# Cross attention's maxima and sums by way of memory in eleven of sixteen batches, in a decoder layer on one Trainium2 core

## The chip, the core and the metric

The kernel runs on one core of a Trainium2 chip. The core has five engines with an instruction queue each. TensorE multiplies matrices and writes to PSUM. VectorE, ScalarE and GpSimd work on rows of 128 partitions. SyncE (SP in the profile) does no arithmetic here and only issues transfers. Sixteen DMA engines carry the transfers between the chip's memory (HBM, "memory" from here on) and SBUF, the core's working memory. [...]

The metric is the device time of one execution in microseconds. A profile of one more execution names every instruction with its start and its end. In the profile PE is TensorE's matmuls, PEld its weight loads, DVE is VectorE, ACT ScalarE, POOL GpSimd.

## The reference

One layer of a decoder over x of shape (16, 128, 512), all float32, in three stages that each end in a residual sum and a layer norm:

```python
x = _layernorm(x + _L0_attn_ref(x, ...))              # retention, 16 heads of 32
x = _layernorm(x + _L0_xattn_ref(x, ctx_2048, ..., 64))  # banded cross attention
x = _layernorm(x + _L0_ffn_ref(x, ...))               # 16 routed rows of each batch
```

The second stage is what the change is about. It works on each batch for itself, with the 512 columns as positions and the 128 rows as features, in 8 heads of 16 features:

```python
scores = einsum('bqhd,bkhd->bhqk', q, k) / sqrt(d)
scores = where(abs(q_pos - k_pos) <= 64, scores, neg)
attn = softmax(scores, axis=-1)
o = einsum('bhqk,bkhd->bqhd', attn, v).reshape(n, t, e)
o = transpose(o @ w_out.T + b_out)
y = relu(o) * encodings
out = einsum('nit,io->not', y, w_ct) + b_ct
```

The third stage picks 16 rows of each batch by a router score, runs attention (16 heads of 128, 8 key heads) and a gated feed-forward of width 2048 on the 256 picked rows, and puts them back.

## The kernel before

**Stages and order.** Retention goes in eight groups of two batches: projections `Q`, `K`, `V` and the gate `G` (`rotated` L549, `values` L568, `gates` L577), scores `R` (`retain` L598), their use `Y` (`weigh` L624), the group norm (`variance`, `normalise`) and the output projection `O` (`finish` L667). Cross attention goes in 32 units m: a unit is one batch n and one head group hg of four heads. `start_ff` then frees retention's weights, loads those of the feed-forward, and the last part follows.

The order of all this is written out by hand. `PLACES`, `ENDS`, `FIRST`, `ONCE` and `FF_PLACES` hold a number for each stage of each step ("s0", "low", "w0", "div" ...), in units of which four make a group. `in_order` sorts these numbers and issues the steps in that order; a step that yields is continued at its next number. So the numbers fix each engine's instruction order, the order on the DMA queues too, and nothing else schedules.

**A cross-attention unit.** The four heads of a unit lie at partitions 0, 32, 64 and 96. Of each 32 partitions, 16 hold the head's features (rows 0 to 15 in head group 0, 16 to 31 in group 1), and one of the others is free: `FREE = (16, 0)`.

1. `project` (L689) makes qT and kT of a batch, 128x512, one tile for each head group. The free row of kT holds 1.
2. `scores` (s0, s1): 8 program matmuls for each half of the positions (L719) into four PSUM banks, then eight masked maxima on VectorE (L727), one of each head and 128 positions. Each lands in a column of the tile x_mx (128 positions in the partitions).
3. `lower` (low): the maxima have to stand in the free row of qT, with the positions along the row. Four TensorE transposes of 128x128 against the identity (L738) bring x_mx there, and VectorE forms x_qa = qT - transposed (L740). As the free row of kT is 1, the next product subtracts each position's maximum by itself.
4. `weights` (w0, w1): the same products the other way round (L753), so that the keys are in the partitions, exp on ScalarE (L758), the band cut out on GpSimd (L764).
5. `attend` (av): values times weights (L775). V (`project_v`, x_va) has a column of ones, so that one row of each 32 of the result is the sum of the weights. ScalarE copies it to xu (L780).
6. `divide` (div): four transposes (L788) put the positions into partitions, VectorE takes the sums' reciprocals (L791) and multiplies (L794) into xo.
7. `turn`: when both head groups are there, four more transposes (L801) turn xo back, ScalarE adds the bias b_v (L803).
8. `project_out` (L808, L810, L812), `settle` (L818 to L842: second layer norm, router score, plain output to memory) and `rank` (L853 to L868: which rows are picked).

The eight PSUM banks are one pool, `banks`, which every step above shares. The feed-forward opens pools of its own after it; its first `frot_ps` of the queries (`rotary`, L966; ScalarE L974 and L976, VectorE L972) has to wait until the old banks are read out.

**Queues.** SP issues nearly all transfers in the order of the places: xT and x of a group (`load`), the encodings (`encoder`, L699), the plain output (L842), the weights. ScalarE's queue issues a few at the start. A transfer that waits holds up those behind it on its queue.

## Time and profile before

| what | value |
|---|---|
| three timed runs | 879.86, 881.25, 881.61 us; median 881.25 |
| the profiled execution | 879.75 us, of which the span from first to last instruction is 878.0 |
| granted TensorE clock, mean over the span | 0.993 |
| instructions | 17870 |
| DMA | 51.31 MB, 16 engines busy for 18% of the span |

How it is read: busy time is the union of an engine's instructions. A group's line gives where it stands in the code, engine, operation, what it writes and reads, how often; after the bar the busy time in us and the mean duration of one in ns; after the second bar the engine's idle time just before, and what ended it. Matmuls overlap each other in the pipeline, so a group's busy time is more than the time by which it moves what comes after. float32 matmuls appear as two instructions each, transposes as one. "PEclk" and the column after the five engines in the table by stages are the granted clock of TensorE, 1.00 being full. A DMA line gives the size and the median time from its issue to its landing.

### The profile page before, as it was taken

How to read it: one execution, taken by the hardware profiler on the slowest of the kernel's cores; microseconds unless marked ns; L12 is line 12 of the kernel's file. 1: busy time of each engine (PE TensorE's matmuls, PEld its weight loads, DVE VectorE, ACT ScalarE, POOL GpSimd, SP SyncE). 2: the span in 40 equal slices, each digit the busy share in tenths (PEclk: the TensorE clock that was granted, in tenths of full speed). 3: DMA queues.
4: the chain of work that ended last, by engine and by line, in shares of the span. 5: the costliest groups of instructions: out<-in, count | busy, mean ns of one | idle time of the engine just before them, and what ended most of it. 6: DMA issues, size and time to landing. Idle time of an engine off the chain costs nothing.

```text
span 878.0 us, 17870 instructions
## 1 busy us (share of the span) xinstructions
PE 835.0 (95%) x6940; PEld 582.5 (66%) x6940; DVE 527.6 (60%) x1789; ACT 392.7 (45%) x768; POOL 346.2 (39%) x508
## 2 busy tenths in 40 slices
PE   7999999999999999999999999998988699999996
PEld 5666767766766775677667757565553587658862
DVE  4645665666676777767677877888853256412101
ACT  0323645635555564545456456575532256521100
POOL 2444454355354745544552744446531121000001
PEclk9999999999999999999999999999999899999999
DMA  9500100100001001011000000019100522242500
GB/s 300 171 1 5 58 1 1 62 1 2 26 18 56 13 26 61 13 40 46 3 13 26 13 14 26 13 35 327 36 27 14 190 96 71 74 144 96 187 5 24
DMA packets 29619, 51.31 MB, mean 58 GB/s; under 512 B 4448, under 2 KB 7776, under 8 KB 29536
## 3 DMA queue, kind: packets, MB, share of 16 engines
q1 hardware_dynamic: 27024, 47.81, 16.2%
q10 hardware_dynamic: 2352, 1.84, 0.7%
q8 instruction: 55, 0.90, 0.4%
q0 software_dynamic: 160, 0.52, 0.2%
q14 instruction: 28, 0.23, 0.1%
HBM read 45.45 MB, written 4.72 MB: 57 GB/s over the span
## 4 chain that ended last, share of the span: by engine, by line
PE 83%; DVE 6%; ACT 3%; issue 3%; DMA 2%; POOL 1%; POOLq 0%; ACTq 0%; SPq 0%; DVEq 0%
PE xt_ps L753 7%; PE o_ps L667 6%; PE gu_ps L1154 6%; PE g_ps L577 6%; PE xs_ps L719 6%; PE v_ps L568 6%; PE q_ps L549 6%; PE xav_ps L775 6%; PE k_ps L549 6%; PE down_ps L1166 3%; PE wo_ps L1129 3%; PE xqk_ps L689 3%; PE frot_ps L966 2%; PE ret_ps L598 2%; PE y_ps L624 2%
## 5 line engine op out<-in xcount | busy, mean ns | idle before, releaser
L727 DVE CUSTOM_DVE_ANT_0 x_masked<-xs_ps,x_band 128x192 f32<-128x192 f32 (+1 forms) x512 | 200.1, 391 | 103.1 <-PE xs_ps L719 64.6
L764 POOL TENSOR_SCALAR_AFFINE_SELECT xp_t<-xp_t 128x512 f32<-128x512 f32 (+1 forms) x256 | 142.1, 591 | 101.4 <-ACT xp_t L758 101.3
L758 ACT ACTIVATE xp_t<-xt_ps 128x448 f32<-128x448 f32 x256 | 118.6, 550 | 60.3 <-PE xt_ps L753 60.2
L753 PE MATMUL xt_ps<-x_qa,x_kT 32*128 32x192 f32 (+1 forms) x1024 | 68.5, 374 | 2.0 <-DVE x_qa L740 1.5
L719 PE MATMUL xs_ps<-x_kT,x_qT 32*128 32x192 f32 (+1 forms) x1024 | 68.7, 358 | 1.2 <-ACT x_qT L692 0.6
L549 PE MATMUL q_ps<-xT,w_W_Q 128*128 128x256 f32 x256 | 60.5, 390 | 5.1 <-DMA w_W_Q<-in_W_Q 5.1
L753 PEld LDWEIGHTS xt_ps<-x_qa,x_kT 32*128 32x128 f32 x1024 | 45.2, 184 | 27.7 <-issue 13.0
L577 PE MATMUL g_ps<-xT,w_W_G 128*128 128x256 f32 x256 | 59.4, 385 | 1.6 <-DMA w_W_G<-in_W_G 1.6
L568 PE MATMUL v_ps<-w_W_V,xT 128*128 128x512 f32 x128 | 58.2, 597 | 1.1 <-DVE w_W_V L484 1.1
L549 PEld LDWEIGHTS q_ps<-xT,w_W_Q 128*128 128x128 f32 x256 | 48.8, 194 | 15.6 <-DMA xT<-in_xT 5.0
L549 PE MATMUL k_ps<-xT,w_W_K 128*128 128x256 f32 x256 | 58.6, 382 | 0.0
L667 PE MATMUL o_ps<-w_W_O,y 128*128 128x512 f32 x128 | 58.4, 599 | 0.0
L719 PEld LDWEIGHTS xs_ps<-x_kT,x_qT 32*128 32x128 f32 x1024 | 52.1, 184 | 9.0 <-DVE x_mx L727 3.1
L775 PE MATMUL xav_ps<-xp_t,x_va 128*32 128x192 f32 (+1 forms) x1024 | 55.0, 355 | 1.8 <-DVE rank L865 0.9
L577 PEld LDWEIGHTS g_ps<-xT,w_W_G 128*128 128x128 f32 x256 | 47.4, 190 | 11.5 <-DMA w_W_G<-in_W_G 2.0
L549 PEld LDWEIGHTS k_ps<-xT,w_W_K 128*128 128x128 f32 x256 | 47.9, 190 | 9.4 <-issue 1.6
L608 POOL TENSOR_SCALAR_AFFINE_SELECT rt<-rt 128x2048 f32<-128x2048 f32 x16 | 32.1, 2005 | 54.7 <-ACT rt L603 50.3
L775 PEld LDWEIGHTS xav_ps<-xp_t,x_va 128*32 128x32 f32 x1024 | 31.1, 110 | 21.9 <-issue 6.0
L979 POOL TENSOR_TENSOR other<-other,ff_sin 128x512 f32<-128x512 f32 x12 | 15.4, 1287 | 72.6 <-ACT other L976 72.6
L568 PEld LDWEIGHTS v_ps<-w_W_V,xT 128*128 128x128 f32 x128 | 23.5, 190 | 28.7 <-issue 25.4
L727 DVE DVE_READ_ACCUMULATOR2_ANT x_mx<- 128x1 f32 x512 | 42.4, 83 | 0.0
L667 PEld LDWEIGHTS o_ps<-w_W_O,y 128*128 128x128 f32 x128 | 23.4, 190 | 27.0 <-issue 23.3
(199 smaller groups left out, 1488.2 us busy)
## 6 DMA issues: line engine op xcount, KB each, us to landing
xp<-in_x SPq DMA_DIRECT2D x16, 256.0 KB, 4.4
enc<-in_ctx SPq DMA_DIRECT2D x16, 256.0 KB, 2.6
out<-z_plain SPq DMA_DIRECT2D x16, 256.0 KB, 2.0
wq<-in_wq SPq DMA_DIRECT2D x4, 1024.0 KB, 5.2
wo<-in_wo SPq DMA_DIRECT2D x4, 1024.0 KB, 6.1
w_gate<-in_w_gate SPq DMA_DIRECT2D x4, 1024.0 KB, 5.1
w_up<-in_w_up SPq DMA_DIRECT2D x4, 1024.0 KB, 5.2
w_down<-in_w_down SPq DMA_DIRECT2D x4, 1024.0 KB, 6.0
```

The source lines that it names most:

```text
L549: nc.tensor.matmul(ps[:, i * GT:(i + 1) * GT], w[wname][:, kc, hg * P:(hg + 1) * P], st["xT"][:, kc, :], start=(kc == 0), stop=(kc == KC - 1))
L568: nc.tensor.matmul(ps, state[g]["xT"][:, kc, b * S:(b + 1) * S], w["W_V"][:, kc, :], start=(kc == 0), stop=(kc == KC - 1))
L577: nc.tensor.matmul(ps[:, i * GT:(i + 1) * GT], w["W_G"][:, kc, hg * P:(hg + 1) * P], state[g]["xT"][:, kc, :], start=(kc == 0), stop=(kc = ...
L608: nc.gpsimd.affine_select(out=v, in_=v, pattern=[[0, 8 * GB], [1, S]], base=0, channel_multiplier=-1, compare_op=ALU.is_ge, fill=0.0)
L667: nc.tensor.matmul(ps, st["y"][:, kc, b * S:(b + 1) * S], w["W_O"][:, kc, :], start=(kc == 0), stop=(kc == KC - 1))
L719: nc.tensor.matmul(ps[j][:, OFF[c]:OFF[c] + LEN[c]], qT[hs, c * P:(c + 1) * P], kT[hs, LO[c]:LO[c] + LEN[c]], start=True, stop=True)
L727: nc.vector.tensor_tensor_reduce(out=junk[:, 0:LEN[c]], in0=ps[j][:, OFF[c]:OFF[c] + LEN[c]], in1=band[:, SEEN[c]:SEEN[c] + LEN[c]], scale ...
L753: nc.tensor.matmul(ps[j][:, OFF[c]:OFF[c] + LEN[c]], kT[hs, c * P:(c + 1) * P], qa[hs, LO[c]:LO[c] + LEN[c]], start=True, stop=True)
L758: nc.scalar.activation(p[:, j, :], ps[j][:, 0:448], AF.Exp, scale=XD ** -0.5)
L764: nc.gpsimd.affine_select(out=v, in_=v, pattern=[[0, 4], [sign, b - a]], base=a if sign == 1 else P - a, channel_multiplier=-sign, compare ...
L775: nc.tensor.matmul(ps[32 * j:32 * (j + 1), LO[c]:LO[c] + LEN[c]], va[:, c, hg * 4 + j, :], p[c // 2][:, j, OFF[c]:OFF[c] + LEN[c]], start= ...
L1154: nc.tensor.matmul(ps[:, j * n:(j + 1) * n], loaded[f"{w}{q}"][:, kc, at:at + P], ff["x1", "T"][:, kc, lo:hi], start=(kc == 0), stop=(kc = ...
```

## The change

In batches 2 to 12 (`IN_MEMORY`) the maxima and the sums go to their rows through memory; batches 0, 1, 13, 14 and 15 keep TensorE's transposes.

- `lower`: the maxima are kept as 16 columns of a 128x32 tile. VectorE transposes its 32x32 blocks into x_mT, SP writes that to memory (128 runs of 128 bytes) and, at a later place, reads it back straight into the four free rows of qT (4 rows of 2 KB). qT itself is used in `weights`; there are four qT buffers in place of two and no x_qa. The free row of kT now holds -1, and the batches with transposes add in place of subtracting.
- `attend`: SP writes the four rows of sums to memory. The values of head group 1 stand at rows 16 to 31, and there are three xu buffers in place of one.
- `divide`: SP reads the sums as 32x64, VectorE takes the reciprocals, SP writes them and reads them back spread over 32 partitions each (256 KB, x_rb), VectorE multiplies xu by them and by a mask. Each of the four pieces has a place of its own.
- `turn`: GpSimd adds the two head groups; there is no transpose.
- b_v is folded into the output's bias by one small matmul at the start; w_out and b_v are loaded in eight pieces each, with their rows in the new order. V is copied out of PSUM in two pieces.
- xpos and w_mean stand in tiles that are used later for something else.
- All places are other numbers, the feed-forward's too. TensorE's order in the feed-forward, from the queries on, is the same as before. Just before it, the second batch half's first key block stands ahead of its value block in place of behind it.

The core of the diff, without the numbers:

```diff
+IN_MEMORY = range(2, 13)
...
         def lower(m):
             n, hg = divmod(m, 2)
-            mx = mxs[hg].rearrange("p c j w -> p c (j w)")
-            ps = bank("xmx_ps")
-            for c in range(NQ):
-                nc.tensor.transpose(ps[:, c * P:(c + 1) * P], mx[:, c, :], ident)
-            qa = xk.tile([P, D], F32, name="x_qa")
-            nc.vector.tensor_tensor(qa, cross[n].pop(("q", hg)), ps, ALU.subtract)
-            unit[m] = dict(qa=qa, p={})
+            unit[m] = dict(qa=cross[n].pop(("q", hg)), p={})
+            if n not in IN_MEMORY:
...
+                return
+            mT = small.tile([P, 32], F32, name="x_mT", bufs=2)
+            nc.vector.transpose(mT, mxs[hg])
+            m_d = dram.tile([32, NQ, 32], F32, name="x_mT_d")
+            nc.sync.dma_start(out=m_d.rearrange("jc b q -> b jc q"), in_=mT)
+            yield
+            nc.sync.dma_start(out=unit[m]["qa"][FREE[hg]::32, :],
+                              in_=m_d[0:4 * NQ].rearrange("(j c) b q -> j (c b q)", j=4))
...
-            u = xk.tile([P, D], F32, name="xu", bufs=1)
+            u = xk.tile([P, D], F32, name="xu", bufs=3)
             nc.scalar.copy(u, ps)
             unit[m]["u"] = u
+            if n in IN_MEMORY:
+                sum_d = dram.tile([4, D], F32, name="sum_d")
+                nc.sync.dma_start(out=sum_d, in_=u[FREE[hg]::32, :])
+                unit[m]["sum"] = sum_d
...
         def divide(m):
...
+            few = D // 8
+            r = xk.tile([32, few], F32, name="x_r", bufs=1)
+            nc.sync.dma_start(out=r, in_=unit[m]["sum"].rearrange("j (q k) -> (j q) k", k=few))
+            yield
+            nc.vector.reciprocal(r, r)
+            inv_d = dram.tile([4, D], F32, name="inv_d")
+            nc.sync.dma_start(out=inv_d.rearrange("j (q k) -> (j q) k", k=few), in_=r)
+            yield
+            rb = xk.tile([P, D], F32, name="x_rb", bufs=1)
+            nc.sync.dma_start(out=rb, in_=bc(inv_d, 1, 32))
+            yield
             u = unit.pop(m)["u"]
+            nc.vector.scalar_tensor_tensor(u, u, ours[:, hg:hg + 1], rb, ALU.mult, ALU.mult)
+            cross[n]["o", hg] = u
...
         def turn(n):
+            o = cross[n]["oT"] = xk.tile([P, D], F32, name="xo", bufs=1)
+            if n in IN_MEMORY:
+                nc.gpsimd.tensor_tensor(o, cross[n]["o", 0], cross[n]["o", 1], ALU.add)
+                return
...
+            ps = bank("bias_ps")
+            nc.tensor.matmul(ps[:, 0:1], w_out, b_v, start=True, stop=True)
+            nc.vector.tensor_tensor(b_out, b_out, ps[:, 0:1], ALU.add)
```

## The prediction

> **What bounds the kernel now.** I read the page's busy table and its slices, then the chain that ended last, then the busy time by stages, TensorE's groups and waits, and last the DMA list. Busy times and slices (40 of 21.95 us each):

> ```profile
> PE 835.0 (95%) x6940; PEld 582.5 (66%) x6940; DVE 527.6 (60%) x1789; ACT 392.7 (45%) x768; POOL 346.2 (39%) x508
> PE   7999999999999999999999999998988699999996
> DVE  4645665666676777767677877888853256412101
> PE 83%; DVE 6%; ACT 3%; issue 3%; DMA 2%; POOL 1%; POOLq 0%; ACTq 0%; SPq 0%; DVEq 0%
> ```

> The third line above is VectorE by slices, the fourth the chain by engine. TensorE bounds everything: 83% of the chain, full slices except near the start, at 590 to 700 us and at the end. Stages (us; busy of each engine, then clock):

> ```profile
> 100.00:500.00 400.00, 399.37 (x3893) 278.94 (x3893) 281.69 (x974) 211.31 (x376) 204.28 (x296) 1.00 0.07 23
> 500.00:580.00 80.00, 79.09 (x818) 51.67 (x817) 62.93 (x238) 46.28 (x84) 36.39 (x61) 1.00 0.06 21
> 580.00:650.00 70.00, 61.10 (x636) 38.26 (x635) 55.95 (x217) 39.25 (x74) 40.09 (x74) 1.00 0.35 125
> 650.00:700.00 50.00, 38.09 (x198) 25.47 (x197) 19.04 (x53) 13.93 (x37) 7.91 (x11) 0.91 0.27 90
> ```

> From 100 to 500 us TensorE waits 0.6 us in all, VectorE works 70%. From 580 us on (only cross attention left; I call it the drain) VectorE is at 80% and TensorE idles 9 us; from 650 to 700 it idles 12 us, 8.0 of them in one wait. The transposes, and that wait:

> ```profile
> L738 PE MATMUL xmx_ps<-consts,x_mx 128*128 128x128 f32 x128 | 20.6, 279 | 0.2
> L788 PE MATMUL xut_ps<-consts,xu 128*128 128x128 f32 x128 | 19.8, 278 | 1.1 <-ACT xu L780 1.1
> L801 PE MATMUL xoT_ps<-consts,xo 128*128 128x128 f32 x64 | 9.8, 276 | 0.9 <-DVE xo L794 0.9
> PE frot_ps L966 <- ACT other L976: 9.1, 2, 8.0
> ```

> How four transposes stand in TensorE's time (start, duration):

> ```profile
> 311.81 0.60 PE L738 MATMUL xmx_ps<-consts,x_mx 128*128 128x128 f32 x4
> 312.25 0.60 PE L788 MATMUL xut_ps<-consts,xu 128*128 128x128 f32 x4
> 312.78 0.32 PE L624 MATMUL y_ps<-rt,v 128*32 128x128 f32 x4
> 322.30 0.66 PE L738 MATMUL xmx_ps<-consts,x_mx 128*128 128x128 f32 x4
> 322.79 1.06 PE L706 MATMUL xv_ps<-x_w_v,xp 128*128 128x128 f32 x8
> 331.25 0.60 PE L801 MATMUL xoT_ps<-consts,xo 128*128 128x128 f32 x4
> 331.69 0.59 PE L667 MATMUL o_ps<-w_W_O,y 128*128 128x512 f32 x1
> ```

> Durations overlap; a group of four holds TensorE 0.44, 0.53, 0.49 and 0.44 us from its start to the next group's, mean 0.475.

> **The sum's base.** The profiled execution took 879.75 us (span 878.0, 1.75 around it), 1.5 under the median of the three timed runs.

> **1. Transposes removed.** Eleven batches are 22 units (batch and head group). Each loses four transposes of maxima and four of sums, each batch four in `turn`: 22 x 8 + 11 x 4 = 220, or 55 groups. By starts 55 x 0.475 = 26.1 us; by the rows' busy time 176 x 0.158 + 44 x 0.153 = 34.5 us, which counts overlapped tails. I take 26 and keep 34.5 as the end. One matmul for the bias is added, 0.2 us (nearest: a one-column matmul, 210 ns). [...]

> **2. Other engines, per unit.** VectorE loses the subtraction (L740, 675 ns), the reciprocal (L791, 252) and the product (L794, 424): 22 x 1.35 = 29.7 us. It gains a 32x32-block transpose of 128x32 (bounds 83 ns, the accumulator read, and 220, the 128x128 copy; I take 0.15), a reciprocal of 64 columns (between 252 ns for 16 and 948 for 128; 0.55) and a product of 128x512 out of SBUF (between 0.75, L1143, and twice 0.757, L659 with 256 columns; 1.0, near L834's 0.87): 22 x 1.7 = 37. Net +8 us on 527.6, range +2 to +20: hidden under TensorE until the drain. ScalarE loses eleven evictions of 692 ns and evicts V in two pieces (0 to +0.6 us, 16 times), GpSimd gains eleven additions of 1.3 us; both have over 40% free.

> **3. Memory trips, maxima.** Between the last score matmul and the first `weights` matmul of a unit now lie: eight masked maxima (8 x (0.39 + 0.083) = 3.8 us), the transpose 0.15, two issues on SP (0.34 each) and two landings, the second issued only when the first has landed. No row has such a trip. Bounds from the list of DMAs:

> ```profile
> out<-z_plain SPq DMA_DIRECT2D x16, 256.0 KB, 2.0
> enc<-in_ctx SPq DMA_DIRECT2D x16, 256.0 KB, 2.6
> x_b_k<-in_b_k SPq DMA_DIRECT2D x1, 0.5 KB, 2.9
> xp<-in_x SPq DMA_DIRECT2D x16, 256.0 KB, 4.4
> ```

> A lone one lands in 2.0 to 2.9 us, 4.4 behind others. I take 2.0 to 2.9, since these are small and the engines 5% busy: the chain is 8.6 to 10.4 us, 13.4 at 4.4. Against it I counted, in the changed program's order, the TensorE work that stands in between, by starts: in unit 6 it is eight `rotated` matmuls, eight scores, sixteen `attend`, one output and four `finish`, 10.7 us; in unit 19 10.2; in the other twenty 11.9 to 21.4, the median of all 15.7. So two of 22 units are tight. In the 2nd to 7th groups the waits cost 0 to 3 us; I take 2. Nothing is queued behind a waiting `weights` matmul but all of TensorE, so such a wait counts in full.

> [...]

> **4. Memory trips, sums.** After `attend`: copy 0.59, four hops (the last writes 256 KB: 2.6 to 5.7, the row of w_router), reciprocal 0.55, product 1.0, both groups added 1.3: 13 to 19 us with issues. TensorE work up to the output matmul is 25 to 77 us, except in batch 12's second group: 14. There I take 1 us (0 to 4). On VectorE the reciprocal and the product may wait for their DMA and hold back masked maxima queued behind; a few reciprocals stand only 1 to 2 us after their load's place.

> **5. SP's queue.** 22 x 6 = 132 DMAs and 14 small ones at the start, each 0.34 us of issue, all in one order. Three per unit wait for the DMA before them, 2 to 2.9 us each, so SP is held 4 x (6 x 0.34 + 3 x 2.5) = 38 us of each group of some 80. Behind them stand xT, x, enc and z transfers, each placed many us ahead of its reader; I cost that at nothing. At the start the 14 extra issues (0.43 each) move the last b_v piece from 31 to about 37 us; its matmul comes near 39.

> **6. Places.** Start: R0's scores now precede the gates and the tables precede centring; VectorE and GpSimd rows put R0 at 23.3 us, where 1.65 us were lost before, and V is due at 33.5 as before: 0 (-1 to +2). Join with the feed-forward: the 8.0 us wait was for two evictions of key heads; now one of them has a V block beside it, and the other takes 4 x 1.16 = 4.7 us: -3 (-3.3 to 0). Drain: in the last 131 us of TensorE work before the first queries VectorE has 125 us by rows where it had 118, with 20 us of TensorE idling before; +4 (0 to +12).

> The clock bears on both: the granted clock was 0.91 from 650 to 700 us, and a `fv` block that began at 673.28, after waits of 2.11 and 0.78, took 8.83 us where its twin took 7.03. The waits between 40 and 650 us, all under 1.0 us, left it at 1.00. So a wait of some 2 us can cost 1.8 more; one such is inside the +4 of the drain. [...]

> **Sum:** 879.75 - 26.1 + 0.2 + 2 + 1 - 3 + 4 = 857.9; taken as 858.

> **Rivals.** *A. Memory slower than the gaps, ends slower.* The chain of step 3 grows to C, and a unit waits C less its gap. Summed over the 22 gaps that is 1 us at 11, 3 at 12, 16 at 14 and 25 at 15: from C = 15 the saving is eaten. That needs hops of 5 us, or VectorE or SP lagging by 5. For it: the 4.4 us row, SP held for half of its time, VectorE at 70 to 80%. Against: 2.0 to 2.9 alone. At 5.5 us a hop C is 15.6 and the stalls are 31 us in place of my 2: 887. *B. Drain bound by VectorE:* its end of +12 and half of A's 16: 858 + 8 + 6 = 872. *C. The rows' price is right:* 858 - 8.4 = 849.6, and with no drain loss 845.6. *D. The change does not move TensorE's time*, as when VectorE already bounds 500 to 650 us: 880; against it are 79.09 of 80 us.

> **Chances.** Forecast (850 to 866) 0.60; C 0.12; B (866 to 879) 0.14; D 0.02; A (over 883) 0.12. About 0.2% (1.8 us) is what a measurement can tell from no change. Faster is forecast, C and B: 0.86; same 0.02; slower 0.12. The range of eight in ten leaves out A and a little below: 845 to 878; the forecast's own is 850 to 866.

> **What would show it.** Right: TensorE's busy time near 805 to 810 us, 0.99 of 100 to 500 us still busy, x_mT_d and x_qT landings of 2 to 3 us, no wait of `weights` on a DMA over 2 us in total. Step 6: the frot wait near 5 us, TensorE idle in the drain near 13. Wrong: `weights`, xout or masked maxima waiting on DMA for tens of us; VectorE at nine tenths over several slices with TensorE at eight.

## The result and the profile after

The changed kernel takes 874.54 us (median of 4 runs, 872.29 to 875.26) against 881.26 for the kernel before, a ratio of 0.9922 with a 95% interval of 0.9901 to 0.9944: 7 us faster. The forecast was 858, 23 us faster. The direction held. The time lies in the wide range (845 to 878) and outside the forecast's own (850 to 866): two thirds of the forecast gain did not come. Every ratio below is to runs of the kernel before taken alongside (their medians lie between 881.3 and 883.1 us), and a difference between two changed kernels is the difference of their ratios.

The profiled execution took 875.26 us, 4.5 under that of the kernel before. First the lines of the page of the changed kernel that answer to those shown of before: busy time of the engines, slices of TensorE and VectorE, the clock that TensorE was granted by slices, and the chain that ended last.

```profile
PE 833.2 (95%) x6722; PEld 573.4 (66%) x6722; DVE 524.1 (60%) x1790; ACT 384.0 (44%) x773; POOL 364.9 (42%) x523
PE   7899999999999999999999999989878799999996
DVE  3744676576677676877777888767764266411111
PEclk9999999999999999999999999989897899999999
PE 86%; DVE 6%; DMA 3%; ACT 2%; issue 1%; POOL 1%; POOLq 0%; ACTq 0%; DVEq 0%
```

218 matmuls fewer are recorded (6940 to 6722), yet TensorE's busy time fell by 1.8 us only. The reader should distrust that: a block of 32 records of key heads (L1050, 128x128) is busy for 6.27 us from 671.67 us on, nearly all of it at half clock, and one of the same shape for 3.73 from 684.64 on, at full; and records overlap there, at 275 ns each with 112 ns from one start to the next. The clock's line has four slices under nine tenths; that of before, which follows, has one:

```profile
PEclk9999999999999999999999999999999899999999
```

The stages, as before (us; busy of TensorE, its loads, VectorE, ScalarE, GpSimd; then the clock, the DMA share and GB/s):

```profile
100.00:500.00 400.00, 399.75 (x3845) 273.71 (x3840) 284.38 (x1013) 211.83 (x395) 224.96 (x317) 1.00 0.12 36
500.00:580.00 80.00, 76.73 (x752) 46.94 (x754) 64.04 (x239) 45.43 (x86) 43.00 (x68) 0.96 0.12 37
580.00:650.00 70.00, 61.81 (x589) 38.55 (x582) 52.34 (x187) 33.51 (x66) 36.71 (x68) 0.92 0.39 133
650.00:700.00 50.00, 40.63 (x183) 28.23 (x184) 18.72 (x53) 14.53 (x39) 6.90 (x7) 0.83 0.28 90
```

From 500 us on the clock is 0.96, 0.92 and 0.83, where it was 1.00, 1.00 and 0.91. Mean clock over the span: 0.977 against 0.993. (1 - clock) x span says how much full-speed clock is missing: 20.1 us against 6.1.

The transposes that are left, by groups of one shape, and TensorE's waits:

```profile
L789 PE MATMUL xmx_ps<-consts,x_wide_mx 128*128 128x128 f32 x40 | 6.1, 276 | 0.0
L853 PE MATMUL xut_ps<-consts,xu 128*128 128x128 f32 x40 | 6.1, 280 | 0.4 <-ACT xu L839 0.4
L886 PE MATMUL xoT_ps<-consts,x_rb 128*128 128x128 f32 x20 | 3.2, 283 | 1.0 <-DVE x_rb L860 1.0
...
PE frot_ps L1050 <- ACT other L1060: 5.8, 2, 4.7
PE hT_ps L1021 <- DVE rms_h L1017: 4.7, 2, 2.5
PE xs_ps L764 <- DVE x_qT L790: 3.0, 2, 2.0
PE ret_ps L641 <- POOL ret_kT L604: 2.1, 1, 2.1
```

The transposes are gone: from start to start (idle time left out) those of maxima took 16.4 us and take 5.1, those of sums 16.4 and 5.1, those of the turning 8.2 and 2.6. That is 28.1 us less, for a forecast of 26.1. So the question is where 21 to 24 us went.

**Where they went.** To see this I counted every matmul at the mean time from its start to the next one's that its kind has in the profile of before, idle time left out, and summed it over all matmuls but the transposes. The sum says how far TensorE is with its real work. How far each kernel is ahead of the kernel before at the same moment, in us of such work (kernels below the first are from the experiments; the figures hold to about 1 us, those of the last row to 2, depending on how kinds are told apart):

| at (us) | 100 | 500 | 550 | 600 | 650 | 720 |
|---|---|---|---|---|---|---|
| changed kernel | -0.7 | 11.0 | 12.5 | 5.2 | 3.4 | 3.1 |
| no_trips | -0.7 | 10.5 | 12.1 | 10.4 | 7.9 | 9.6 |
| before_less | -0.5 | 10.0 | 10.4 | 8.6 | 11.6 | 9.0 |
| batch12_transposed | 1.2 | 13.1 | 12.8 | 11.6 | 9.3 | 11.0 |
| thin_exps | 1.6 | 16.9 | 16.6 | 9.4 | 8.8 | 11.4 |
| all_transposed | -0.7 | -26.5 | -29.7 | -30.5 | -23.8 | -34.3 |

Two losses stand in the first row. Up to 500 us 21.4 us of transposes are gone, but the changed kernel is 11.0 ahead: some 10 us are lost in a stretch in which the clock is 1.00 and TensorE's recorded waits are a quarter of a microsecond. Between 550 and 650 us, in the drain, 9 of the 12.5 us are given back. (The 2 us between the first and the fourth row at 100 us are one stretch of half clock, 24.85 to 28.26 us in the changed kernel, after the wait of 2.1 us for ret_ps at 24 us; some executions have it, see the part on the clock.)

### The profile page after: what moved, and what is told of

Read it like the earlier page. It is cut to its first block, busy times and chain, and to the rows that moved or that the text cites. A ratio compares the mean times of both kernels' runs of the same rounds, so it can differ in the third digit from the quotient of the medians.

```text
span 873.6 us, 17752 instructions
## 1 busy us (share of the span) xinstructions
PE 833.2 (95%) x6722; PEld 573.4 (66%) x6722; DVE 524.1 (60%) x1790; ACT 384.0 (44%) x773; POOL 364.9 (42%) x523
## 4 chain that ended last, share of the span: by engine, by line
PE 86%; DVE 6%; DMA 3%; ACT 2%; issue 1%; POOL 1%; POOLq 0%; ACTq 0%; DVEq 0%
PE xt_ps L812 7%; PE g_ps L620 7%; PE xs_ps L764 7%; PE v_ps L611 6%; PE gu_ps L1238 6%; PE o_ps L710 6%; PE xav_ps L834 6%; PE q_ps L592 6%; PE k_ps L592 6%; PE frot_ps L1050 3%; PE down_ps L1250 3%; PE wo_ps L1213 3%; PE xqk_ps L732 3%; PE ret_ps L641 2%; PE y_ps L667 2%; PE fv_ps L1031 2%
## 5 line engine op out<-in xcount | busy, mean ns | idle before, releaser
L823 POOL TENSOR_SCALAR_AFFINE_SELECT xp_t<-xp_t 128x512 f32<-128x512 f32 (+1 forms) x256 | 146.7, 610 | 90.8 <-ACT xp_t L817 79.4
L764 PE MATMUL xs_ps<-x_kT,x_qT 32*128 32x256 f32 (+1 forms) x1024 | 76.4, 370 | 5.9 <-DVE x_qT L790 3.0
L812 PE MATMUL xt_ps<-x_qT,x_kT 32*128 32x192 f32 (+1 forms) x1024 | 73.8, 383 | 0.6 <-DVE x_qT L790 0.6
L812 PEld LDWEIGHTS xt_ps<-x_qT,x_kT 32*128 32x128 f32 x1024 | 49.4, 190 | 27.2 <-issue 13.1
L834 PE MATMUL xav_ps<-xp_t,x_va 128*32 128x192 f32 (+1 forms) x1024 | 57.6, 367 | 0.0
L646 ACT COPY rt<-ret_ps 128x512 f32<-128x512 f32 x64 | 32.9, 600 | 38.3 <-PE ret_ps L641 38.2
L834 PEld LDWEIGHTS xav_ps<-xp_t,x_va 128*32 128x32 f32 x1024 | 31.3, 113 | 25.5 <-issue 7.8
L1063 POOL TENSOR_TENSOR other<-other,ff_sin 128x512 f32<-128x512 f32 x12 | 15.6, 1302 | 71.7 <-ACT other L1060 71.7
## 6 DMA issues: line engine op xcount, KB each, us to landing
x_rb<-inv_d SPq DMA_DIRECT2D x22, 256.0 KB
xp<-in_x SPq DMA_DIRECT2D x16, 256.0 KB
enc<-in_ctx SPq DMA_DIRECT2D x16, 256.0 KB
out<-z_plain SPq DMA_DIRECT2D x16, 256.0 KB
```

Of the source, the lines that this page charges most:

```text
L646: nc.scalar.copy(rt[:, j].rearrange("p g b s -> p (g b s)"), sc[j])
L764: nc.tensor.matmul(ps[j][:, OFF[c]:OFF[c] + LEN[c]], qT[hs, c * P:(c + 1) * P], kT[hs, LO[c]:LO[c] + LEN[c]], start=True, stop=True)
L812: nc.tensor.matmul(ps[j][:, OFF[c]:OFF[c] + LEN[c]], kT[hs, c * P:(c + 1) * P], qa[hs, LO[c]:LO[c] + LEN[c]], start=True, stop=True)
L823: nc.gpsimd.affine_select(out=v, in_=v, pattern=[[0, 4], [sign, b - a]], base=a if sign == 1 else P - a, channel_multiplier=-sign, compare ...
L834: nc.tensor.matmul(ps[32 * j:32 * (j + 1), LO[c]:LO[c] + LEN[c]], va[:, c, hg * 4 + j, :], p[c // 2][:, j, OFF[c]:OFF[c] + LEN[c]], start= ...
```

## The experiments

The first theory said that the memory trips cost what was lost, most of it in the drain, where the product of batch 12's sums waits at the head of VectorE. These are VectorE's and SP's waits on trips in the changed kernel (us in total, times, longest):

```profile
DVE xu L876 <- DMA x_rb<-inv_d: 8.2, 6, 2.7
DVE xu L876 <- DMA sum_d<-xu: 3.6, 1, 3.6
...
SPq L866 <- DMA sum_d<-xu: 24.9, 19, 4.4
SPq L799 <- DMA x_mT_d<-x_mT: 16.5, 17, 2.9
SPq L873 <- DMA inv_d<-x_r: 10.0, 9, 2.7
```

And VectorE's and TensorE's instructions where it shows (start, duration; idle time before and what ended it in brackets):

```profile
571.73 1.13 DVE L876 SCALAR_TENSOR_TENSOR xu<-xu,x_ours,x_rb 128x512 f32<-128x512 f32 x1 [2.72 <-DMA x_rb<-inv_d]
572.78 0.68 DVE L790 TENSOR_TENSOR x_qT<-x_qT,xmx_ps 128x512 f32<-128x512 f32 x1
...
577.04 0.54 DVE L868 RECIPROCAL x_r<-x_r 32x64 f32<-32x64 f32 x1
...
585.73 0.75 DVE L876 SCALAR_TENSOR_TENSOR xu<-xu,x_ours,x_rb 128x512 f32<-128x512 f32 x1 [1.10 <-DMA x_rb<-inv_d]
586.40 0.68 DVE L790 TENSOR_TENSOR x_qT<-x_qT,xmx_ps 128x512 f32<-128x512 f32 x1
...
587.14 1.16 PE L764 MATMUL xs_ps<-x_kT,x_qT 32*128 32x192 f32 x14 [2.01 <-DVE x_qT L790]
```

VectorE stands still for 2.72 and 1.10 us because a product waits for its row. The addition L790 behind it is late: the transposes that it reads were done at 569.31 and 583.26 us (L789, 0.64 us from 568.67 and 0.60 from 582.66), and it starts at 572.78 and 586.40, each time after the product. TensorE, which waits for that addition, idles 0.94 and 2.01 us.

**no_trips: all trips left out.**

```diff
-            m_d = dram.tile([32, NQ, 32], F32, name="x_mT_d")
-            nc.sync.dma_start(out=m_d.rearrange("jc b q -> b jc q"), in_=mT)
             yield
-            nc.sync.dma_start(out=unit[m]["qa"][FREE[hg]::32, :], ...
...
-            nc.vector.reciprocal(r, r)
+            nc.vector.reciprocal(r, w_r[0:32, 0:few])
...
-            rb = xk.tile([P, D], F32, name="x_rb", bufs=1)
-            nc.sync.dma_start(out=rb, in_=bc(inv_d, 1, 32))
+            rb = w_r
```

> The changed program without its memory trips: maxima stay in their tile and sums in theirs, so nothing is written to memory and nothing is read back; the block transpose, the reciprocal and the product stay, on a constant tile; the rows' maxima and the division are left out of what is computed. Theory 1 (the trips hold VectorE and SP, TensorE waits for what stands behind them, most of it at 548 to 640 us, and the clock halves there): the changed kernel's 874.5 less the 15 to 20 us that were given back, 855 to 860. Theory 2 (the new places and VectorE's own load give it back, trips or not): 871 to 875. Theory 3 (taking out the transposes saves little, since other matmuls slow down in their place): 872 to 875.

865.07 us, ratio 0.9799 (0.977 to 0.9828): 11 us faster than the changed kernel, not 15 to 20. The table shows why: up to 550 us it is where the changed kernel is, to 0.5 us. Before the drain the trips cost nothing that shows, and SP's waits of 51 us are hidden. After 550 us this kernel keeps 10 to 8 of its 12 us. So theory 1 holds for the drain and fails for the rest; 10 us at 100 to 500 us are lost without any trip.

**all_transposed, batch12_transposed, product_later.**

```diff
-IN_MEMORY = range(2, 13)
+IN_MEMORY = range(0)          # all_transposed; x_rb has two buffers, xu two
+IN_MEMORY = range(2, 12)      # batch12_transposed
...
-            (2.8923, 3.4873, 13.643, 28.5999),
+            (3.55, 3.75, 13.643, 28.5999),      # product_later: ENDS[6]["div"], last stage
```

> The changed program's places, all sixteen batches with transposes on TensorE (220 more of them, by starts 28.1 us), with one tile more for x_rb and one less for xu. Theory 1: the places cost nothing by themselves, so 858 without trips and transposes plus 26 to 28, 884 to 888, no longer waits of 1 us or more at 548 to 640. Theory 2: the places cost some 15 us in any case: 895 to 905. Theory 3: 880 to 883.

> Only batch 12 goes back to transposes (20 of them, 2.4 us by starts); places as in the changed kernel. Theory 1, as the two units of batch 12 are those whose product waited 3.6 and 2.7 us for its row at 555 to 575 us: the waits of TensorE behind the product and the two half-clock stretches at 574 and 588 us go; 874.5 + 2.4 less 6 to 12: 865 to 871. Theory 2: 877.

> Only the place of the product of batch 12's two units moves, from 2.89 and 3.49 to 3.55 and 3.75 (units of some 20 us), so that VectorE comes to it when the row has landed. Theory 1: VectorE's waits on x_rb at 571 and 586 us go, with them the half clock at 574 and 588 us: 868 to 872. Theory 2: 874 to 876, since VectorE's work is only moved.

all_transposed took 920.8 us, ratio 1.0433 (1.0402 to 1.0463), more than any theory gave. It loses 26 us by 500 us: the places put `lower` soon after the maxima, since a block transpose on VectorE can wait there; a transposing on TensorE at that place makes TensorE wait for VectorE (15.2 us in nine waits in this row, 10.4 of them by 500 us; the rest of the 26 us is not traced to its places):

```profile
PE xmx_ps L789 <- DVE x_wide_mx L776: 15.2, 9, 4.4
```

So places and trips belong together, and the test of "places alone" says little on either.

batch12_transposed took 865.6 us, ratio 0.981 (0.9783 to 0.9837), 10 us faster than the changed kernel though TensorE has 20 transposes more. In the table it keeps 11.6 us at 600 us, where the changed kernel has 5.2. The scores' wait for x_qT, 3.0 us in the changed kernel, is not in its list, and VectorE still waits 5.4 us for rows, with no wait of over 1 us in TensorE's list behind it. Batch 12 in memory costs 10 us, or up to 12 if its 20 transposes are worth the 2.4 us of their spacing. (Of the waits in VectorE's rows above, the 3.6 us are those of batch 11's second unit, at 555 us, not of batch 12's as the expectation has it; batch 12's two products are the ones shown at 571.73 and 585.73.)

product_later took 873.13, ratio 0.9909 (0.9878 to 0.9941): no gain that can be told from none. The wait moved on:

```profile
PE xout_ps L892 <- POOL xo L882: 6.6, 1, 6.6
...
DVE xu L876 <- DMA x_rb<-inv_d: 10.4, 6, 5.4
```

x_rb has one buffer. With the first unit's product later, that buffer was held for longer; a product now waited 5.4 us for its row (2.72 and 1.10 for these two in the changed kernel), then the output matmul 6.6.

**sums12_transposed, maxima12_transposed, product_of_25_later, batches_11_12_transposed.** Half of batch 12 at a time, a milder move of the product, and one batch more.

```diff
-IN_MEMORY = range(2, 13)
+MAXIMA, SUMS = range(2, 13), range(2, 12)      # sums12_transposed
+MAXIMA, SUMS = range(2, 12), range(2, 13)      # maxima12_transposed
+IN_MEMORY = range(2, 11)                       # batches_11_12_transposed
...
-            (2.8923, 3.4873, 13.643, 28.5999),
+            (2.95, 3.70, 13.643, 28.5999),      # product_of_25_later
```

> Batch 12's maxima go through memory as in the changed kernel, its sums and its turning by transposes (12 more, about 1.5 us). If what batch 12 costs is the trip of its sums (the product at the head of VectorE, waiting for its row): the gain of batch12_transposed over the changed kernel, 9 us, stays and 1 us of transposes is spared, 864 to 866. If it is the trip of its maxima: 874 to 876.

> The reverse: batch 12's maxima by transposes (8 more, 1 us), its sums through memory. If the sums' trip is the cost: 873 to 876, with the product's waits at 555 to 586 us as in the changed kernel. If the maxima's: 864 to 867.

> Only the products of batch 12: the first unit's from 2.89 to 2.95, the second's from 3.49 to 3.70, since with the first at 3.55 the second row found its one buffer held and landed late (the output matmul waited 6.6 us). If the wait of VectorE is what batch 12 costs, a place 4 us later takes 1 to 2 of the three waits: 869 to 872. If the trip is simply longer than the TensorE work that is left, the wait moves on to the output matmul: 873 to 876.

> Batches 11 and 12 go back to transposes, beside batch 12 alone (865.6). If the trips cost only where they run out of TensorE's cover, in batch 12: 865.6 + 2.6, 868. If batch 11's second unit (its product waited 3.59 us for its row at 555 us in the changed kernel) costs as well: 860 to 864.

sums12_transposed: 864.29, ratio 0.9829 (0.9794 to 0.9864), as expected if the sums' trip is the cost. maxima12_transposed: 869.66, ratio 0.9858 (0.9835 to 0.988), where 873 to 876 was expected. The products did not wait as before: at 550 to 600 us they waited 3.3 us, where it was 7.4. So either the maxima's trip has a part of its own in the cost, or taking it out lets the sums' rows come in time; this run does not tell the two apart. product_of_25_later: 871.49, ratio 0.9854 (0.9818 to 0.989), so moving both products, by 0.06 and 0.21 of a unit of some 20 us, gains about 6 us by the ratio; its six runs lie between 863.63 (clock 0.990) and 875.6 (clock 0.973), of which more below. batches_11_12_transposed: 876.05, ratio 0.992 (0.9904 to 0.9936), 10 us behind batch12_transposed: batch 11's transposing at its new place waits 4.71 us for VectorE's maxima, and the clock halves at 509 us, within that wait (0.96 over 500 to 580 us):

```profile
510.63 0.87 PE L789 MATMUL xmx_ps<-consts,x_wide_mx 128*128 128x128 f32 x2 [4.71 <-DVE x_wide_mx L776]
```

**before_less and after_plus: the transposes by themselves.** One takes the 220 transposes out of the kernel before and puts nothing in their place, the other puts 220 dead ones into the changed kernel.

```diff
# before_less, in divide; lower and turn in the same way
-            ps = bank("xut_ps")
-            for c in range(NQ):
-                nc.tensor.transpose(ps[:, c * P:(c + 1) * P], u[:, c * P:(c + 1) * P], ident)
+            if n in LESS:
+                ps = u
+            else:
+                ...
# after_plus, in divide; lower and turn in the same way
+            ps = bank("xut_ps")
+            for c in range(NQ):
+                nc.tensor.transpose(ps[:, c * P:(c + 1) * P], ident, ident)
             few = D // 8
```

> The kernel before, its places and all its other instructions, without the 220 transposes of batches 2 to 12 and without anything in their place: the subtraction, the reciprocal and the product read tiles that are there in any case, and the maxima, the sums' turning and the last turning are left out of what is computed. It prices the removal by itself. Theory S (a group of four frees its 0.475 to 0.51 us wherever it stood; the 10 us that the changed kernel loses at 100 to 500 us in pieces of under 1 us belong to its new places): 852 to 856. Theory P (about half of what a removed group frees is taken by TensorE's waits for its banks, whatever the places): 863 to 868. At 100 to 500 us the first gains about 20 us on the kernel before, the second about 10.

> The changed kernel with the 220 transposes of its eleven batches added again as dead work (of a constant, into a bank of their own, at the place of the block transpose, of the sums' first load and of the turning); nothing waits for them but TensorE's order and the ring of banks. Theory S: 874.5 + 26 to 28, 900 to 903. Theory P: part of them falls into waits that are there, 886 to 892.

before_less: 869.95 us, ratio 0.9859 (0.9844 to 0.9874), 12.4 us for 220 transposes that held TensorE 28 us. At 500 us it is 10.0 ahead, as far as the changed kernel. That is theory P in size: about half of what goes, in places that were made for the transposes, is lost again. But it is not lost as in the changed kernel. At 100 to 500 us TensorE idles 5.4 us here, 4.7 of them in four waits for x_qa, a tile that the changed kernel does not have (there it idles 0.25 us); the other half has no recorded wait. The row of the waits over the whole span, and the stage:

```profile
PE xt_ps L757 <- DVE x_qa L744: 7.6, 7, 2.1
...
100.00:500.00 400.00, 394.59 (x3816) 269.95 (x3814) 297.85 (x1004) 212.75 (x382) 215.94 (x303) 1.00 0.07 23
```

after_plus: 891.38, ratio 1.0094 (1.0073 to 1.0114), 15 us over the changed kernel for 28 us of dead work: in the range that P gave. The table's arithmetic is less kind to P. From 100 to 500 us this kernel falls 5.6 us behind the kernel before, with the same number of transposes, while the changed kernel gains 11.7; so the dead transposes cost 17 of their 21 us there. If a dead transpose costs what a real one did, the 10 us lost at 100 to 500 us have two parts in the changed kernel: 5.6 us belong to its order, transposes or not, and 4 to their going. In the order of the kernel before all 10 belong to their going, half of them as waits for x_qa. That both kernels are some 10 us ahead at 500 us is thus not one cause seen twice.

**thin_exps and thin_maxima: which engine TensorE runs into.**

```diff
-                nc.scalar.activation(p[:, j, :], ps[j][:, 0:448], AF.Exp, scale=XD ** -0.5)
+                few = 224 if n in IN_MEMORY else 448                       # thin_exps
+                nc.scalar.activation(p[:, j, 0:few], ps[j][:, 0:few], AF.Exp, scale=XD ** -0.5)
...
+            few = lambda c: LEN[c] // 2 if n in IN_MEMORY else LEN[c]      # thin_maxima
```

> The changed kernel with the exponentials of its eleven batches over 224 of 448 columns, the others set to one by GpSimd; half of the exponentials is left out of what is computed. ScalarE then empties a bank in about 0.3 in place of 0.46 us and has some 35 us less to do in all. Theory B (the loss at 100 to 500 us is TensorE coming too early for banks that ScalarE still empties, 0.18 us at a time): TensorE is 4 to 8 us further at 500 us, 866 to 871 in the end. Theory O (the spacing has another cause): within 1.5 us of the changed kernel at 500 us, 873 to 876.

> The changed kernel with the masked maxima of its eleven batches over the middle half of their columns (the other half is left out of the maxima), which takes some 0.13 us from each of 352, 45 us from VectorE. Theory 1 (batch 12's reciprocals and products come late since VectorE lags): the reciprocals start 3 us earlier or more, the products' waits fall under 2 us in all, and at 550 to 650 us some 6 of the 9 us come back: 864 to 869. If the trips are too long even with VectorE in time: 872 to 875. At 100 to 500 us theory B expects 0 to 3 us from it.

From 100 to 500 us thin_exps gains 15.3 us on the kernel before, the changed kernel 11.7, thin_maxima 11.8 and no_trips 11.2. So ScalarE's emptying of banks is worth 3.6 of the 10 us, just under the 4 to 8 that theory B gave, VectorE's maxima none, the trips none. One place where it shows is the spreading of the variances (L696), which needs four banks at once; ScalarE and TensorE in the changed kernel:

```profile
248.06 1.41 ACT L817 ACTIVATE xp_t<-xt_ps 128x448 f32<-128x448 f32 x3
249.33 0.62 ACT L839 COPY xu<-xav_ps 128x512 f32<-128x512 f32 x1
249.79 1.04 ACT L817 ACTIVATE xp_t<-xt_ps 128x448 f32<-128x448 f32 x2
...
248.87 1.84 PE L696 MATMUL spread_ps<-gn_rs,spread 32*128 32x128 f32 x15
```

The group has sixteen small matmuls, four to a bank. From the first start to the last they take 1.68 us here, and also at 322 and 396 us; in the undisturbed groups they take 0.47 to 0.48. The first matmul on the second, third and fourth bank starts at 249.09, 249.52 and 250.00 us, each 0.05 to 0.06 us after ScalarE has ended an instruction (249.03, 249.47, 249.95). In thin_exps the same three groups take 0.99 us. Within the groups of this line TensorE spends 6.1 us at 100 to 500 us, where it spent 3.1; in thin_exps 4.4. None of these waits is long enough to show as idle time. The other 6 of the 10 us are spread over scores (1.5 us), weights (about 1) and the seams between groups; what makes them is left open.

In total thin_exps took 871.42 us, ratio 0.9889 (0.9867 to 0.9911), which is hardly clear of the changed kernel's 0.9922, since its lead of 16.6 us at 550 falls to 8.8 in the drain. thin_maxima took 868.97, ratio 0.9862 (0.9839 to 0.9885): 5 us, nearly all of it after 550 us. So VectorE's lag is a part of the drain's loss. Theory 1 wanted the products' waits under 2 us in all; those for x_rb are 8.3 us, and the last three (549 to 578 us) have 3.7 where they had 7.4. So an earlier VectorE alone does not hide the trips.

**The clock.** The runs of one kernel differ, and they differ with the clock: after_plus took 887.91 us at 0.987 and 894.92 at 0.978. In these profiles the clock's records come in stretches of 3.41 us, at full or at half (in the changed kernel the half ones that hold matmuls last 3.41 or 6.83 us). How much half clock slows a matmul: the 128x256 ones of the queries (L1050) follow each other by 427 ns up to 697.1 us, at half clock, and by 216 ns after it, at full. I put the stretches of the twenty profiles that lie wholly between 60 and 760 us in classes by how long TensorE idled in them, and looked at the next stretch:

| idle in a stretch of 3.41 us at full clock | stretches | next at half clock |
|---|---|---|
| under 0.25 us | 3587 | 0 |
| 0.25 to 1.0 | 243 | 22 |
| 1.0 to 2.0 | 91 | 20 |
| 2.0 and more | 40 | 40 |

Half clock holds for one or two stretches, once for three (product_later, at 581 us). Where the borders of the stretches fall went with it as well, in the one wait that I compared: TensorE's wait for ret_ps at 24 us was followed by half clock in the changed kernel, where 2.13 us of it lie in one stretch, and not in batch12_transposed, where the wait is longer (2.5 us) but a border cuts it into 1.60 and 0.90. In the changed kernel half clock came seven times, 37.6 us with 34.0 us of matmul time in them; in the kernel before twice, 10.2 us with 7.3. Half of the difference, 13 us, is what it can cost, an estimate by the 427 and 216 ns. 17.0 of the 34.0 us lie between 550 and 650 us, where the kernel before has none: that is 8.5 us, against the 9 us that are given back in the drain (a little more waiting and fewer transposes nearly cancel). It is tested, behind the drain, by keeping TensorE at work in waits that are there in any case:

```diff
+        def fill(count):
+            ps = bank("fill_ps")
+            for _ in range(count):
+                nc.tensor.matmul(ps, ident, c[:, 0:D], start=True, stop=True)
...
+            if what == "xs":
+                fill(5)          # 2 in the half-filled kernels (in that of before at i = 1 alone)
             ps = ff["bank"]("hT_ps")
...
+            if (i, j) == (1, 1):
+                fill(10)         # 5; in the kernel before 17 and 8
...
+            if n > 13:
+                fill(2)          # half-filled: 1, for n = 14 alone; not in the kernel before
             ps = bank("slot_ps")
```

> The changed kernel with 24 dead matmuls of 128x512 (0.44 us each) put where TensorE waits behind the drain in any case: five ahead of each transposing of the gathered rows (waits of 2.47 and 2.25 us), two ahead of each of the last two slot matmuls (0.90, 0.71), ten after the last key heads (4.74). They do nothing but keep TensorE at work. Theory C (the clock: stretches with 1 to 2.3 us of idle time are followed by half clock, and the changed kernel has more of them): the half clock at 656, 670 and 690 us goes (17 us of it), 6 to 8 us of matmul time come back, less some 1.5 us where a dead matmul outlasts its wait: 868 to 870, and a clock above 0.98. Theory W (the waits themselves cost, the clock is only their sign): 874 to 876.

> The same 24 dead matmuls in sums12_transposed (864.3), whose waits there are 2.46, 1.25, 0.71, 2.25 and 4.75 us. Theory C: 857 to 861, faster than every kernel so far. Theory W: 864 to 866.

> The kernel before with 27 dead matmuls: five ahead of each transposing of the gathered rows (2.11 us of waiting at the second), seventeen after the last key heads (8.01). Theory C: its two half-clock stretches (10.2 us, 7.3 us of matmul time in them) go: 3 us faster, with 1 to 2 us lost ahead of the first transposing where nothing waits; 0.9965 to 1.000 of the kernel before. Theory W: 1.000 to 1.004.

after_filled 875.31, ratio 0.9922 (0.9899 to 0.9944); sums12_filled 867.0, 0.984 (0.9814 to 0.9865); before_filled 888.81, 1.0085 (1.0067 to 1.0102). No gain, and no test of the theories, since I had the filling's size wrong. It was twice what I thought; a matmul of this shape is recorded as two (in sums12_filled 24 of them stand as 48):

```profile
L421 PE MATMUL fill_ps<-consts x48: 592/592/676, 630.5 to 686.2; 128*128 128x512 f32 x48
```

At 0.89 us each the filling outlasted the waits by 10 us (24 times 0.89 against 11.4 us of waits in sums12_transposed). With a filling that fits:

> The same ten in the changed kernel, where the half clock at 656, 670 and 690 us (17 us) goes and that of the drain at 574, 588 and 615 us stays. Theory C: 866 to 869. Theory W: 874 to 876.

> In sums12_filled a dead matmul of 128x512 took 0.89 us, not 0.44 (two passes), so 24 of them were 21 us of work against 11.5 us of waits, and 10 us of it stood uncovered; the time still rose by 3 us alone. Here there are ten: two ahead of each transposing of the gathered rows, one ahead of a slot matmul, five after the last key heads, 8.9 us into waits of 2.46, 2.25, 1.25 and 4.75. Theory C: nothing uncovered, the half clock at 633, 647, 661 and 681 us (13.6 us) goes and some 6 us come back: 857 to 860, a clock of 0.995. Theory W: 864 to 866.

> The kernel before with ten dead matmuls: two ahead of the second transposing (2.11 us of waiting), eight after the last key heads (8.01). Theory C: its half clock (10.2 us in the profile) goes, 3 to 5 us come back: 0.994 to 0.997 of the kernel before. Theory W: 1.000.

after_half_filled took 866.24 us, ratio 0.9815 (0.9786 to 0.9843): ten matmuls that compute nothing make the changed kernel 9 us faster. sums12_half_filled took 860.86, ratio 0.9759 (0.9733 to 0.9786), the fastest of all and 21 us under the kernel before. before_half_filled took 877.71, ratio 0.9956 (0.9936 to 0.9975). That is theory C (sums12_half_filled is 0.9 us above its range and 3 us under that of theory W). The stage at 650 to 700 us of after_half_filled, and the clock's slices of sums12_half_filled:

```profile
650.00:700.00 50.00, 47.57 (x221) 31.53 (x221) 22.39 (x65) 17.92 (x45) 9.88 (x10) 1.00 0.33 111
```

```profile
PEclk9999999999999999999999999999899999999999
```

The clock is 1.00 in that stage, where the changed kernel had 0.83, and 221 matmul records stand in it, 16 of them of dead matmuls, for 183.

## Why the prediction was right or wrong

**Step 1, the transposes removed (-26.1): the step that failed.** The spacing was right: 28.1 us went from TensorE's queue. That they come out of the time was an inference from 0.6 us of recorded waits at 100 to 500 us, and it was wrong by half: before_less, which does only this, gained 12.4 us, and the changed kernel keeps 11 of 21 us at 500 us. TensorE bounds the kernel at its present pace; with 21 us taken out of 400 it comes too early. In the order of before half of the loss is waiting for x_qa (4.7 us at 100 to 500 us). In the changed kernel 3.6 of the 10 us are ScalarE's banks (thin_exps), 5.6 go with the new order (after_plus), and the two may overlap; what makes the rest is open. Neither of the two prices that I weighed, 119 ns a transpose by spacing (128 over all transposes) or 157 by the rows' busy time, could have told this: the price per transpose was not the question.

**Step 2, other engines (hidden).** VectorE was to gain 8 us. By its rows it gained 34.6 (product 18.8, reciprocal 11.5, block transpose 4.3) and lost 29.8, 5 net. Hidden until the drain, as said.

**Steps 3 and 5, the maxima's trips (+2) and SP's queue (0).** Right up to the drain, and 2 us too dear there. No `weights` matmul waits for a DMA, and no_trips is no further at 500 us, though SP waits 51 us on trips. SP's longest wait for the store of a unit's maxima was 2.9 us, where I took 2.0 to 2.9 for a landing. In the drain batch 12's maxima may have a cost of their own: with them transposed the kernel gained 6 us (maxima12_transposed), which is not told apart from what it does for the sums.

**Step 4, the sums' trips (+1, range 0 to 4): wrong in size.** It named batch 12's second group as the tight one and said that the product might hold back what is queued on VectorE behind it. That is what happened, in both groups of batch 12, and it cost 8 to 10 us (sums12_transposed, batch12_transposed), some ten times the term. My 0 to 4 counted the trip against TensorE's work. The wait stood on VectorE, with 75 to 80% of its time taken there, and from there it reached TensorE through another batch's addition (0.94 and 2.01 us); half clock stands there too, from 574.39 and from 588.05 us.

**Step 6, places.** The wait for the key heads went from 8.0 to 4.7 us, as the -3 had it. Nothing is left of it in the table, which stands at 3.4 us at 650 and at 3.1 at 720: half clock at 650 to 720 us covers 13.6 us of matmul time in the changed kernel and 7.3 in the kernel before, which costs 3.2. The drain was to cost 4 us with one half clock of 1.8 inside; TensorE gave back 9 us there, batch 12's among them; its half clock there is worth 8.5.

**The clock.** I had from one `fv` block that a wait of some 2 us can cost 1.8 us more, and then allowed one such wait. In the changed kernel half clock came seven times. In the twenty profiles 2.0 us of idle time or more in 3.41 us were followed by it 40 times of 40, in one gap or in several (1.44 and 0.78 us ahead of 673.81 us in the kernel before), and 1.0 to 2.0 us in 20 of 91. So half clock is a price of the order of the whole change: ten dead matmuls took 9 us off the changed kernel and 4 off the kernel before, though half clock of the drain was still there (at 575, 603 and 613 us in after_half_filled).

**Rivals.** A (memory slower than the gaps) and D fell. C fell. B, the drain bound by VectorE, had 866 to 879 and a chance of 0.14; the time lies in it, and thin_maxima (5 us) and batch 12 support its half about the drain. The other half of its sum, waits for the maxima's trips, did not come. That the time lies in B's range is in part luck: no rival had the 10 us that were lost at 100 to 500 us.

**What would show it.** "TensorE's busy time near 805 to 810 us" was the right question: 833.2 was the sign, at first sight, that the removed time had been filled with slower work. The sign for the trips that could be read (no wait of `weights` on a DMA) came out as forecast; the profile gives no landing times for x_mT_d and x_qT.

## What to carry to other kernels

Idle time of next to nothing on the bounding engine does not say that work taken from it is time saved (here 0.6 us idle in 400, 28 us of transposes taken out, 12.4 us saved); take the work out alone, with nothing in its place, and see what is left before costing what replaces it. Here the trips through memory cost nothing that shows while their ends were far away (no_trips is within 0.5 us of the changed kernel at 500 us), and much near the end of the stage (8 to 10 us for batch 12), where the waiting instruction sat at the head of an engine that was already late. In the twenty profiles 2.0 us of waiting or more within one stretch of 3.41 us were followed by half clock for one or two stretches, once for three. Ten matmuls that compute nothing, 8.9 us put into waits that were there, made the changed kernel 9 us faster, where the whole change had made 7.
